# Two output blocks of a fused FFN: copied out of PSUM by ScalarE and added to x by the transfer out

## The chip, the cores and the metric

The kernel runs on one core of a Trainium2 chip. The core has a matrix engine (TensorE, PE in the profile; PEld is its weight load), a vector engine (VectorE, DVE), a scalar engine (ScalarE, ACT), a general engine (GpSimd, POOL) and SyncE (SP), which here only issues DMA transfers. The metric is device time in microseconds: 259.87 us before, the median of three runs (259.43 to 259.95).

## The reference

`x` is 64 batches of 64 rows of 512 numbers, all in 32 bits. Cut to what matters, the reference computes

```
q   = relu(cond @ W3 + b3)                      # 64 x 512, one row a batch
v   = (64 * x + sum of x over the batch's rows) * q
y   = relu(v @ W2 + b2)
out = x + y @ W_base + b_base + (y @ A_s) @ B_s + sum over e of w_e * (y @ A_r[e]) @ B_r[e]
```

Here `w_e` are the two largest of six softmax gates of `y @ W_router + b_router`, the others being zero. The `x +` at the front of `out` is what the change is about.

## The kernel before

The 4096 rows of x are cut into four blocks (k = 0 to 3) of 1024 rows. Everything is held transposed: features on the 128 partitions, rows along the free axis. One block passes through these stages: modulation of x to v, first matmul (W2) to y, a matmul `ph` (L1066) for gates and low-rank factors, and the second matmul (W_base) with the routed part added, then the transfer out.

Both large matmuls use Strassen-Winograd products: a block's matrix is split in two by two, so that seven products (`prod` with numbers 1 to 7) replace eight. In the second matmul, `second` (L658), sums of products accumulate in PSUM banks named x, y, z and w, each with two columns j = 0 and 1 of 128 features. Four result blocks come out: C12 and C22 (features 256 to 511) begin as `with_x("y", ...)` and `with_x("z", ...)`, where DVE adds rows of x to a bank into an SBUF tile, and are completed by `leave` (L690) from bank w. C11 (bank x) and C21 (bank z), features 0 to 255 of the two halves of the rows, are complete in their banks once `routed` (L682) has added the routed part, and leave through `finish` (L687), which is called four times a block.

The rows of x to be added come from `load_rows` (L648): it loads four tiles of 128 x 2 x 512 numbers, 512 KB each, with transfers issued by SP. The tiles have the tags u21, u, u22 and u12, with one buffer each. u22 holds the rows of C11 and u12 those of C21. The same four tags are the scratch tiles of the first matmul (`temps`, L60): in `first_inner` (L431), which does the first matmul of blocks 1 to 3, tag u is p1, u22 is p5, u21 is u and u12 is v7. So the first writer of p5 in block k + 1, the second of the two copies by ACT at L468, waits until the transfers out of u22 in block k are done.

The order of work is written out by hand: each engine runs its instructions in the order in which the code issues them, with waits on semaphores set in between. While block k is in its second matmul, the modulation of block k + 1 (L218 on ACT, with sums on DVE) is handed out from the list `behind` by `share` (L698), nine times in `second`. The counts in `share` hand out all of the modulation's activations by the fourth call, which precedes the first `finish`; the later calls give out DVE's row sums (L269 to L272) and inner sums (L307 to L310), which the next block's first matmul reads. POOL computes `hwd` (L604) from the routed factors, then the steps of `beside[k]` (L1028 in block 0, four additions of `inner_tb` in block 1, eight in block 2), and in the next block the sums `inner_two` and `inner_late` (L307, L550).

The last block's second matmul is another function, `second_inner` (L759), with its own ways out.

Of the kernel before, what the change touches and what calls it, by code (L numbers as in the profile page):

```python
# [11 lines left out]
ALU = mybir.AluOpType  # L12
# [7 lines left out]
TB = 512  # L20
NB = T // (2 * TB)
# [4 lines left out]
KH = NC // 2  # L26
# [11 lines left out]
def adaln_ffn(ctx: ExitStack, tc: tile.TileContext, xa, x0, x1, head, w3, w2, wb, a, bcat, bb, br, outT):  # L38
# [8 lines left out]
    nc = tc.nc  # L47
# [126 lines left out]
    def product(ps, i, j, w, s, start=True):  # L174
        for c in range(KH):
            nc.tensor.matmul(  # L176
                ps, w[i][:, c, ts(j, P)], s[i][:, c, :], start=start and c == 0, stop=c == KH - 1,
                skip_group_check=True,
            )
# [99 lines left out]
    def fill(n):  # L279
        for _ in range(min(n, len(behind))):  # L280
            for step in behind.pop(0):
                step()
# [301 lines left out]
    def weigh(k, ph):  # L584

        nc.vector.tensor_tensor(
            hw[:, :, :GR].rearrange("p s (g r) -> p s g r", r=R),
            ph[:, :, :GR].rearrange("p s (g r) -> p s g r", r=R),
            w.unsqueeze(3).to_broadcast([P, 2 * NS, G, R]),
            ALU.mult,  # L590
        )

    def turn(k):
        pt = ps_h.tile([P, 2 * NS, P], F32, tag="ph", name=f"pt_{k}")
        hwT = small.tile([P, 2, TB], F32, tag="hwT", name=f"hwT_{k}")
        for s in range(2 * NS):
            nc.tensor.transpose(pt[:GB, s, :], hw[:, s, :], ident)  # L597
        for h in range(2):
            nc.scalar.copy(hwT[:GB, h], pt[:GB, ts(h, NS)].rearrange("p s t -> p (s t)"))  # L599
        return hwT  # L600

    def difference(k, hwT):
        hwd = small.tile([P, TB], F32, tag="hwd", name=f"hwd_{k}")
        nc.gpsimd.tensor_tensor(hwd[:GB], hwT[:GB, 0], hwT[:GB, 1], ALU.subtract)  # L604
        return hwd
# [42 lines left out]
    def load_rows(k):  # L648

        res = {}  # L650
        for n, (f, h) in zip(pair_tags[2:3] + pair_tags[:2] + pair_tags[3:], ((1, 0), (1, 1), (0, 0), (0, 1))):
            res[f, h] = tmp.tile([P, KH, TB], F32, tag=n, name=f"x{n}_{k}")
            nc.sync.dma_start(
                res[f, h], x1[k, f * KH : (f + 1) * KH, :, ts(h, TB)].rearrange("c p t -> p c t")
            )
        return res

    def second(k, y, ph, res):  # L658

        sy = sys_[k]  # L660
        ps = {}

        def bank(name, j):
            ps[name, j] = ps_p.tile([P, TB], F32, tag="pp", name=f"o{name}_{k}_{j}")
            return ps[name, j]

        def prod(i, j, name, start=True):
            product(bank(name, j) if start else ps[name, j], i, j, tb, sy, start=start)

        def seed(name, source, j):  # L670
            nc.scalar.copy(bank(name, j), ps[source, j])

        def row(f, h):
            return res[f // KH, h][:, f % KH]

        def with_x(name, j, f, h):

            t = row(f, h)
            nc.vector.tensor_tensor(t, ps[name, j], t, ALU.add)
            return t  # L680

        def routed(name, j, f, hw):  # L682
            nc.tensor.matmul(  # L683
                ps[name, j], bcat_sb[:, ts(f, P)], hw, start=False, stop=True, skip_group_check=True
            )

        def finish(name, j, f, h):  # L687
            nc.sync.dma_start(outT[k, f, h], with_x(name, j, f, h))

        def leave(p, f, h, add):  # L690
            nc.vector.tensor_tensor(add, p, add, ALU.add)
            nc.sync.dma_start(outT[k, f, h], add)


        places = list(range(9, 0, -1))
        most = {9: 4, 8: 5, 7: 6}

        def share():  # L698
            n = places.pop(0)
            left = len(behind) - 13  # L700
            fill(min(left, most.get(n, 6)) if left > 0 else -(-len(behind) // n))

        gate(k, ph)
        prod(1, 0, "x")
        seed("y", "x", 0)
        prod(1, 1, "x")
        seed("y", "x", 1)
        prod(6, 0, "y", start=False)
        seed("z", "y", 0)
        prod(2, 0, "x", start=False)  # L710
        weigh(k, ph)
        u12, u22 = {}, {}
        u12[0] = with_x("y", 0, KH, 0)
        share()
        prod(7, 0, "z", start=False)
        u22[0] = with_x("z", 0, KH, 1)
        prod(6, 1, "y", start=False)
        seed("z", "y", 1)
        u12[1] = with_x("y", 1, KH + 1, 0)
        share()  # L720
        prod(2, 1, "x", start=False)
        prod(7, 1, "z", start=False)
        u22[1] = with_x("z", 1, KH + 1, 1)
        hwT = turn(k)
        hwd = difference(k, hwT)
        for step in beside[k]:
            step()
        share()
        prod(4, 0, "z", start=False)
        prod(5, 0, "w")  # L730
        share()
        routed("x", 0, 0, hwT[:GB, 0])
        finish("x", 0, 0, 0)
        routed("z", 0, 0, hwT[:GB, 1])
        finish("z", 0, 0, 1)

        routed("w", 0, KH, hwT[:GB, 1])
        leave(ps["w", 0], KH, 1, u22[0])
        share()
        prod(5, 1, "w")  # L740
        routed("w", 1, KH + 1, hwT[:GB, 1])
        leave(ps["w", 1], KH + 1, 1, u22[1])
        share()
        routed("x", 1, 1, hwT[:GB, 0])
        finish("x", 1, 1, 0)
        share()
        prod(4, 1, "z", start=False)
        routed("z", 1, 1, hwT[:GB, 1])
        finish("z", 1, 1, 1)
        share()  # L750
        prod(3, 0, "w", start=False)
        routed("w", 0, KH, hwd[:GB])
        leave(ps["w", 0], KH, 0, u12[0])
        share()
        prod(3, 1, "w", start=False)
        routed("w", 1, KH + 1, hwd[:GB])
        leave(ps["w", 1], KH + 1, 0, u12[1])
# [280 lines left out]
    for k in range(NB):  # L1038
# [6 lines left out]
        if k == 1:  # L1045
            wide_sums()
        res = load_rows(k)
        if k == 0:
            load_x(3)
# [79 lines left out]
```

## Time and profile before

The profiled execution took 259.86 us; its span on the core is 258.1 us.

| | before |
|---|---|
| profiled execution, us | 259.86 |
| span, us | 258.1 |
| TensorE busy, us | 252.6 |
| VectorE busy, us | 199.6 |
| ScalarE busy, us | 142.7 |
| GpSimd busy, us | 68.8 |
| mean granted TensorE clock | 0.997 |
| additions of x from PSUM (L679): number, us each | 24, 0.68 |
| stores of `finish` (L688): number, us to landing | 12, 2.0 |
| loads of `load_rows` (L653): number, us to landing | 16, 3.7 |

Blocks begin their first matmul on TensorE at 73.2 (block 1), 134.8 (block 2) and 196.3 us (block 3), and their second at 41.4, 102.8 and 164.3 us (blocks 0 to 2). Busy shares are averages over stages with different limits; where an engine waits, the profile names what ended the wait.

### The profile page before, as it was taken

The numbers are of one execution on the slowest core, as the hardware profiler recorded it, in microseconds if no ns is written. First come the engines' busy times: TensorE is split into PE (matmuls) and PEld (weight loads), VectorE is DVE, ScalarE is ACT, GpSimd is POOL, SyncE is SP. The second block draws the span as 40 slices with busy tenths as digits, with TensorE's granted clock in tenths as the row PEclk, the third lists the DMA queues.
The fourth block names the chain that finished last, engine by engine and source line by source line (L and its number), as shares of the span: only waits on it lengthen the run. The fifth ranks groups of instructions, "written<-read, shape, count | busy, mean of one in ns | idle before, by whom it ended". The sixth has DMA issues, their size and how long they took to land.

```text
span 258.1 us, 3326 instructions
## 1 busy us (share of the span) xinstructions
PE 252.6 (98%) x1034; PEld 170.6 (66%) x1034; DVE 199.6 (77%) x404; ACT 142.7 (55%) x391; POOL 68.8 (27%) x88
## 2 busy tenths in 40 slices
PE   7999999999999999999999999999999999999994
PEld 3755896454468889445448888744446889975783
DVE  2899898789958976967995894996896476887473
ACT  2399587597037897279106889439603527443220
POOL 1000000012008520005104650000920864039950
PEclk9999999999999999999999999999999999999998
DMA  6998729403320035000431023300232003600054
GB/s 174 369 341 297 290 79 379 192 3 122 122 81 0 4 143 183 0 3 0 163 123 41 0 83 118 130 0 3 104 140 81 0 6 128 193 1 3 0 183 142
DMA packets 14675, 28.54 MB, mean 111 GB/s; under 512 B 1489, under 2 KB 3537, under 8 KB 14658
## 3 DMA queue, kind: packets, MB, share of 16 engines
q1 hardware_dynamic: 14370, 28.08, 30.9%
q10 hardware_dynamic: 288, 0.26, 0.3%
q8 instruction: 8, 0.13, 0.2%
q14 instruction: 9, 0.07, 0.1%
HBM read 19.94 MB, written 8.39 MB: 110 GB/s over the span
## 4 chain that ended last, share of the span: by engine, by line
PE 94%; ACT 2%; DMA 2%; SPq 0%; issue 0%; DVE 0%
PE ia L453 13%; PE ph L1066 11%; PE ib L453 10%; PE oz L176 9%; PE ox L176 8%; PE ow L176 8%; PE py L361 5%; PE oy L176 5%; PE ja L820 4%; PE ow L683 4%; PE jb L820 4%; PE ox L683 2%; PE oz L683 2%; DMA w_sb<-in_w_dram 2%; PE yw L176 1%; PE pt L597 1%
## 5 line engine op out<-in xcount | busy, mean ns | idle before, releaser
L218 ACT ACTIVATE x<-x,vsum,nq 128x64 f32<-128x64 f32 x192 | 67.5, 431 | 6.8 <-DVE vsum L214 6.8
L604 POOL TENSOR_TENSOR hwd<-hwT 113x512 f32<-113x512 f32 x4 | 5.6, 1393 | 109.4 <-ACT hwT L599 109.4
L1066 PEld LDWEIGHTS ph<-a_sb,y 128*128 128x128 f32 x256 | 30.3, 192 | 1.3 <-ACT y L347 0.7
L1066 PE MATMUL ph<-a_sb,y 128*128 128x118 f32 x256 | 30.8, 276 | 0.3 <-ACT y L347 0.3
L459 ACT COPY ib<-ia 128x256 f32<-128x256 f32 x21 | 7.6, 361 | 42.3 <-PE ia L453 42.3
L444 DVE TENSOR_TENSOR u<-ib,u 128x256 f32<-128x256 f32 x42 | 16.4, 418 | 18.6 <-PE ib L453 18.5
L176 PE MATMUL ox<-y,wb_sb 128*128 128x512 f32 x48 | 22.1, 593 | 0.0
L444 DVE TENSOR_TENSOR u<-ia,u 128x256 f32<-128x256 f32 (+1 forms) x36 | 16.1, 461 | 2.9 <-ACT u L491 1.6
L347 ACT ACTIVATE y<-u,head_sb 128x256 f32<-128x256 f32 (+1 forms) x30 | 15.8, 584 | 3.8 <-DVE u L419 3.1
L453 PE MATMUL ib<-inner_s,inner_t 128*128 128x256 f32 x60 | 17.8, 384 | 0.0
L213 DVE TENSOR_REDUCE vsum<-x 128x8 f32<-128x512 f32 x24 | 16.2, 675 | 0.0
L176 PEld LDWEIGHTS ox<-y,wb_sb 128*128 128x128 f32 x48 | 8.9, 190 | 10.0 <-issue 9.6
L176 PE MATMUL oz<-sy,tb 128*128 128x512 f32 x32 | 15.2, 599 | 0.0
L361 PE MATMUL py<-v,w_sb 128*128 128x512 f32 (+1 forms) x40 | 14.4, 510 | 0.8 <-DMA w_sb<-in_w_dram 0.8
L176 PE MATMUL oy<-sy,tb 128*128 128x512 f32 x32 | 14.9, 594 | 0.0
L307 POOL TENSOR_TENSOR inner_two<-x 128x256 f32<-128x256 f32 x3 | 2.2, 727 | 45.0 <-PE ib L453 45.0
L462 ACT COPY ib<-ib 128x256 f32<-128x256 f32 x21 | 7.6, 363 | 9.9 <-PE ib L453 9.9
L453 PEld LDWEIGHTS ib<-inner_s,inner_t 128*128 128x128 f32 x60 | 11.2, 190 | 2.2 <-ACT ib L462 0.8
L256 ACT ACTIVATE v<-x,vsum,nq 128x64 f32<-128x64 f32 x32 | 11.0, 430 | 1.9 <-DVE vsum L254 1.9
L361 PEld LDWEIGHTS py<-v,w_sb 128*128 128x128 f32 x40 | 7.4, 190 | 6.5 <-issue 4.5
L176 PE MATMUL oz<-y,tb 128*128 128x512 f32 x24 | 11.3, 592 | 0.0
L176 PE MATMUL ow<-sy,tb 128*128 128x512 f32 x24 | 11.3, 592 | 0.0
(236 smaller groups left out, 545.0 us busy)
## 6 DMA issues: line engine op xcount, KB each, us to landing
xu<-in_x_dram SPq DMA_DIRECT2D x16, 512.0 KB, 3.7
out_dram<-xu SPq DMA_DIRECT2D x29, 256.0 KB, 2.0
x<-in_x_dram SPq DMA_DIRECT2D x12, 512.0 KB, 7.6
x<-in_x_dram SPq DMA_DIRECT2D x7, 256.0 KB, 5.6
w_sb<-in_w_dram SPq DMA_DIRECT2D x4, 256.0 KB, 5.6
wb_sb<-in_wb_dram SPq DMA_DIRECT2D x4, 256.0 KB, 4.8
out_dram<-xu SPq DMA_DIRECT2D x4, 128.0 KB, 1.7
w_sb<-in_w_dram SPq DMA_DIRECT2D x1, 384.0 KB, 5.2
```

Of the source, the lines that this page charges most:

```text
L176: nc.tensor.matmul(ps, w[i][:, c, ts(j, P)], s[i][:, c, :], start=start and c == 0, stop=c == KH - 1, skip_group_check=True,)
L213: nc.vector.tensor_reduce(vsum[:, c, bs], xc, AX.XY, ALU.add)
L218: nc.scalar.activation(x, x, AF.Identity, bias=vsum[:, c, b : b + 1], scale=nq[:, c, b : b + 1])
L256: nc.scalar.activation(v[:, c, :, ts(b, NH)], batches_of(c, b, b + 1)[:, :, 0], AF.Identity, bias=vsum[:, c, b : b + 1], scale=nq[:, c, b ...
L347: nc.scalar.activation(y[:, f, h, cols], src, AF.Relu, bias=b2_sb[:, f : f + 1])
L361: nc.tensor.matmul(p[:, :, lo * NH : hi * NH], w2_sb[:, c, ts(f, P)], v[:, c, :, lo * NH : hi * NH], start=(c == 0 and lo == 0), stop=(c = ...
L444: add = lambda o, a, b: nc.vector.tensor_tensor(o, a, b, ALU.add)
L453: nc.tensor.matmul(bank[b, t][:, cols], t_side(o, n), s_side(o, n), start=n == 1, stop=True, skip_group_check=True,)
L459: nc.scalar.copy(bank["b", t][:, lo], bank["a", t][:, lo])
L683: nc.tensor.matmul(ps[name, j], bcat_sb[:, ts(f, P)], hw, start=False, stop=True, skip_group_check=True)
L820: nc.tensor.matmul(p, w, s, start=start, stop=True, skip_group_check=True)
L1066: nc.tensor.matmul(ph[:, h * NS + s, :HC], y[:, c, h, ts(s, P)], a_sb[:, c, :], start=(c == 0), stop=(c == NC - 1),)
```

## The change

For blocks 0 to 2, `load_rows` no longer loads the rows of x for C11 and C21 into SBUF. SP issues a transfer from x in DRAM to their place in the output in DRAM instead; the two SBUF tiles are still allocated. `finish` has ACT copy the bank into the tile, and POOL issues a transfer that adds the tile to what stands in the output. The other two result blocks, and block 3, are as before.

```
@@ load_rows
             res[f, h] = tmp.tile([P, KH, TB], F32, tag=n, name=f"x{n}_{k}")
+            if f == 0 and k < NB - 1:
+
+                nc.sync.dma_start(outT[k, :KH, h], x1[k, :KH, :, ts(h, TB)])
+                continue
             nc.sync.dma_start(
                 res[f, h], x1[k, f * KH : (f + 1) * KH, :, ts(h, TB)].rearrange("c p t -> p c t")
             )
@@ second
         def finish(name, j, f, h):
-            nc.sync.dma_start(outT[k, f, h], with_x(name, j, f, h))
+            t = row(f, h)
+            nc.scalar.copy(t, ps[name, j])
+            nc.gpsimd.dma_start(outT[k, f, h], t, accum_op=ALU.add)
```

## The prediction

> **What bounds the kernel now.** I read the page's first two parts, then the chain of waits, busy time by stretches, the list of who waited for whom, and last the timeline of ScalarE (ACT), VectorE (DVE) and GpSimd (POOL) around the end of a block. The page first:
>
> ```profile
> span 258.1 us, 3326 instructions
> PE 252.6 (98%) x1034; PEld 170.6 (66%) x1034; DVE 199.6 (77%) x404; ACT 142.7 (55%) x391; POOL 68.8 (27%) x88
> PE 94%; ACT 2%; DMA 2%; SPq 0%; issue 0%; DVE 0%
> ```
>
> TensorE (PE) is busy nearly all the time, and the chain that ended last runs through it for 94% and through DVE for 0%. Shares are averages, so next the stretches of block 1's inner product and of its second matmul, and the last 18 us of the second matmul of blocks 0, 1 and 2 (columns: length, then busy time of each engine, with the number of instructions):
>
> ```profile
> 73.21:102.76 29.55, 29.39 (x164) 25.48 (x163) 21.81 (x47) 23.60 (x66) 10.61 (x12) 1.00 0.23 83
> 102.76:134.75 31.99, 31.99 (x82) 14.46 (x81) 27.31 (x52) 14.06 (x39) 4.67 (x5) 1.00 0.16 58
> ...
> 57.00:75.00 18.00, 18.00 (x47) 8.52 (x46) 17.28 (x24) 6.78 (x22) 2.56 (x2) 1.00 0.27 102
> 118.80:136.50 17.70, 17.70 (x47) 8.38 (x46) 15.88 (x22) 5.46 (x17) 4.67 (x5) 1.00 0.28 104
> 180.40:198.00 17.60, 17.60 (x46) 8.27 (x46) 16.08 (x22) 5.39 (x17) 7.75 (x9) 1.00 0.28 104
> ```
>
> Where the change sits, PE has no idle time at all; DVE is nearly full beside it (17.28 of 18.00), ACT is not (6.78). A full DVE costs only if PE waits for it (us in total, times, longest):
>
> ```profile
> ACT ib L459 <- PE ia L453: 42.3, 15, 12.0
> DVE u L444 <- PE ib L453: 18.5, 13, 2.8
> PEld oz L176 <- ACT oz L671: 1.5, 2, 0.7
> PEld ow L176 <- DVE xu L679: 0.5, 2, 0.2
> ```
>
> The first two lines are engines waiting for PE: ACT idles up to 12.0 us and DVE up to 2.8 us at a block's start. The last is the only wait of PE's weight loads for the additions that go: 0.24 us each, the same gap that the loads beside them show as issue. It costs nothing.
>
> Last, the timeline of ACT, then POOL, where the new copies and transfers will go, and where the next block needs their tile (start, length):
>
> ```profile
> 57.02 6.08 ACT L218 ACTIVATE x<-x,vsum,nq 128x64 f32<-128x64 f32 x18
> 74.11 0.36 ACT L459 COPY ib<-ia 128x256 f32<-128x256 f32 x1 [11.01 <-PE ia L453]
> 75.25 0.38 ACT L468 COPY u<-ia 128x256 f32<-128x256 f32 x1
> 75.98 0.37 ACT L476 COPY u<-ib 128x256 f32<-128x256 f32 x1 [0.36 <-PE ib L453]
> ...
> 187.57 0.90 POOL L170 TENSOR_TENSOR inner_tb<-wb_sb,inner_tb 128x128 f32<-128x128 f32 x1
> 200.54 0.73 POOL L307 TENSOR_TENSOR inner_two<-x 128x256 f32<-128x256 f32 x1 [12.06 <-PE ib L453]
> ```
>
> ACT is empty from 63.10 to 74.11; POOL in the worst block is free from 188.47 to 200.54.
>
> **Removed: twelve DVE additions.** Four in each of blocks 0 to 2 (L679 from `finish`), 0.68 us each, one every 0.60 us when they follow each other: 4 x 0.60 = 2.4 us of DVE a block. None is on the path: before its first work of the next block DVE waits 2.66 us (block 0) or 2.77 us (block 1) for PE, so the 2.4 us lengthen that wait. Worth 0. Bounds: a loss is excluded, since nothing is added to DVE's queue; the gain is at most what PE loses to DVE early in an inner product, weight-load waits of 1.0 us in four and 0.6 us in two for u L444, 0.24 us of each being the ordinary gap, so 1.6 - 6 x 0.24 = 0.2 us.
>
> **Added: twelve ACT copies from PSUM.** The nearest row is the seed copy of the same shape, 0.57 us: 2.3 us a block. `share()` hands out all modulation work before the first `finish` (18 instructions up to 63.10 in block 0, 14 up to 123.61 and 185.14 in the others), so nothing of it queues behind a copy that waits for PE. Block 0: first column of C11 copied 63.10 to 63.67, of C21 to 64.2; second columns when PE ends them, at 65.47 and 68.05, so to 66.1 and 68.7. Cover: ACT's hole of 11 to 12 us; without it, 2.3 us a block. PSUM: the w accumulators reuse the y banks, which DVE empties as before; the banks emptied by the new copies are wanted again only from 73.2. Worth 0.
>
> **Moved: twelve transfers out, from SP's queue to POOL's, as accumulations.** SP loses 12 issues of 0.34 us; nobody waits for SP there, and its other four transfers go out no later. POOL gains 12 issues that wait for the copies. Ahead of them stand hwd and the `beside` steps, behind them the next block's inner_two: at 77.46 in block 0, at 200.54 in block 2. No row of before shows an issue by POOL: at least SP's 0.34 us, at most POOL's longest instruction in this stage, 1.44 us (hwd L604); I take 1.17 us (L1028, POOL's instruction of 256 elements), as POOL's own work is the nearest kind. In block 2 four issues end at 188.47 + 4.7 = 193.2, or 194.2 at the upper bound: before 200.54. Worth 0.
>
> **The new wait.** Tile u22 holds C11 and becomes p5 of the next block: the second ACT copy of L468 (75.25, 136.78, 198.32) may not write it before the second C11 accumulation has read it out and landed. It stood behind a plain store that landed in 2.0 us. Behind it on ACT queue L476 and the seed L462, for which PE waits, so lateness beyond ACT's 0.36 us hole is PE's. Tile u12 (C21) is wanted some 4 us later still.
>
> How long does an accumulation take? No row shows one. The nearest are the transfers of the page (KB each, us from issue to landing) and the rate from 30 to 50 us, in 40 slices:
>
> ```profile
> xu<-in_x_dram SPq DMA_DIRECT2D x16, 512.0 KB, 3.7
> out_dram<-xu SPq DMA_DIRECT2D x29, 256.0 KB, 2.0
> ```
>
> ```profile
> GB/s 213 8 16 25 0 0 0 0 0 0 0 0 0 90 74 332 397 369 410 361 369 348 311 307 311 389 418 430 426 418 418 401 426 418 410 279 188 82 8 0
> ```
>
>  It reads 256 KB from SBUF and 256 KB from DRAM, and writes 256 KB. While eight 512 KB loads ran together (36 to 48 us) the rate was about 418 GB/s: 0.63 us for 256 KB. A plain store lands in 2.0 us, so 1.4 us is latency. Lower bound: like the store, 2.0 us, overlapping. Upper: a 512 KB load (3.7 us) and a store (2.0 us) in sequence, three in a row without overlap, 17.1 us. I take the two reads at the measured rate, 1.3 us each in sequence, and 1.4 us latency once: three take 5.3 us. The stream of 512 KB loads is nearest, because these transfers too are 2 KB rows spread over the same 16 engines and follow each other.
>
> Landing, counted from the end of the first issue: block 0, 64.84 + 5.3 = 70.1 against 75.25; block 1, 124.18 + 1.17 + 5.3 = 130.7 against 136.78; block 2, 188.47 + 1.17 + 5.3 = 194.9 against 198.32. All hidden, by 5.1, 6.1 and 3.4 us. Block 2 gives way first: above (198.32 - 1.4 - 189.64) / 3 = 2.4 us a transfer. At the upper bound lateness is 6.7, 5.7 and 8.4 us: 20.8 less 3 x 0.36, some 20 us: 280 us.
>
> The Trainium skill has a rule against this: "SBUF — State Buffer", section "SBUF: two separate sides", warns that a transfer issued by GpSimd can be starved of descriptors while DVE holds the shared port pair, and a later section prices one at about 3.1 us where 0.62 us was alone. The trace has a neighbour of it: L272 on DVE took 1.75 us beside POOL's hwd where it takes 0.68 us otherwise. By the rule, an estimate, three transfers would come 7.4 us later, and block 2 would lose 4 us; but the same page exempts DVE's two-input additions, and those fill the stretch here.
>
> **Copies of x into DRAM.** They replace two of SP's four loads of 512 KB a block (0.39 us an issue, 3.7 us to land); nothing computes from them until the accumulation 20 us later (issued by 99.55 at the latest in block 1, first used at 124.2). They no longer wait for a tile. At the load's price they are hidden; at a load and a store in sequence, 5.7 us, too. In block 0 the load of x_3 queues behind them, which is used two blocks later. Worth 0.
>
> **End of the program.** SP closes by waiting for every queue's semaphores; the accumulations add up to eight, at 17 to 38 ns each: 0 to 0.3 us. I take 0.05 us, as SP waits 1.8 us for the last store anyway.
>
> **Sum.** Profiled execution 259.86 us (span 258.1, 1.76 around it), the median of three being 259.87: + 0 + 0 + 0 + 0.05 = 259.9 us.
>
> **Rivals.**
> 1. *The accumulations land late and hold ACT at the block's start* (slower; decides above 2.4 us a transfer). For: three 256 KB streams and an adder that no row prices, and issues that start as late as 188.47. Against: 3.4 us of room. At 3.0 us a transfer block 2 is 189.64 + 9.0 + 1.4 - 198.32 - 0.36 = 1.4 us late and blocks 0 and 1 not: 261.3 us. At 3.25 us block 2 is 2.1 us late and block 0 0.4 us: 262.4 us.
> 2. *POOL's first transfer has a starting cost.* For: POOL issues none before. Against: room of 5.1 us in block 0. It shows from 5.1 + 0.36 + 0.5 = 6 us on: 260.4 us.
> 3. *DVE's relief reaches PE.* For: DVE 96% busy at 57 to 75. Against: DVE waits for PE right after. At most 0.2 us by the row above, 259.7 us; to be told from no change it needs a third of PE's 1.5 us wait for ACT's oz seeds as well, which lie ahead of the change's place: 259.2 us.
> 4. *ACT becomes late.* Were modulation behind the copies, up to 2.3 us a block, 266.8 us; its order excludes that.
>
> **How the numbers follow.** About 0.2% (0.5 us) is what a measurement of this kernel tells from no change. Hidden as summed, 0.49 (own range 259.4 to 260.3); rival 1, 0.27; rival 2, 0.06; rival 3, 0.13; rival 4 and other slowings, 0.05. Of the three slower cases' 0.38, 0.02 stays under 0.5 us: slower 0.36, same 0.51, faster 0.13. The range runs to where 1 in 10 is left above (3.25 us a transfer, 262.4 us) and below (259.3 us).
>
> **What would show it.** L679 x12 instead of x24 on DVE and its wait before block starts longer by about 2 us; twelve ACT copies right after the last L218; landing of accumulations under 5 us; the second L468 still 1.14 us after L459 begins. Wrong, if an ACT wait for a transfer appears at L468, if POOL's inner_two starts later than PE lets it, or if PE's stretches of 31.98 us or 29.55 us change.

## The result, and the profile after

The changed kernel takes 260.53 us (median of seven, 260.27 to 261.25), the kernel before beside it 259.87 us (259.35 to 260.24): a ratio of 1.0031 [1.0016, 1.0046]. The change makes the kernel slower by 0.3%, a little more than measurements of it can tell from no change (the interval leaves 1 out by 0.0016). The profiled execution took 260.44 us.

The page of the changed kernel first: span, busy time, engines on the chain that ended last, then two groups and the transfers.

```profile
span 258.7 us, 3333 instructions
...
PE 252.4 (98%) x1034; PEld 170.5 (66%) x1034; DVE 193.0 (75%) x392; ACT 149.1 (58%) x403; POOL 79.3 (31%) x100
...
PE 92%; ACT 2%; DVE 2%; DMA 2%; SPq 0%; issue 0%
...
L694 POOL DMA_DIRECT2D out_dram<-xu x12 | 10.7, 1016 | 11.5 <-ACT xu L693 8.8
...
out_dram<-xu SPq DMA_DIRECT2D x17, 256.0 KB, 2.3
out_dram<-in_x_dram SPq DMA_DIRECT2D x6, 512.0 KB
out_dram<-xu POOLq DMA_DIRECT2D x12, 256.0 KB, 5.1
```

The work moved as the diff says: DVE lost twelve instructions and 6.6 us, ACT gained 6.4 us. PE is as full as before, and DVE, which was on 0% of the chain, is on 2%. Busy time by stretches: block 1's inner product, its second matmul, then block 2's inner product and its second matmul, and last the end of block 0's second matmul.

```profile
72.92:102.53 29.61, 29.45 (x164) 25.49 (x163) 21.29 (x47) 23.60 (x66) 10.59 (x12) 1.00 0.17 60
102.53:134.53 32.00, 32.00 (x82) 14.45 (x81) 25.26 (x48) 16.18 (x43) 8.18 (x9) 1.00 0.36 83
134.53:164.52 29.99, 29.56 (x163) 25.48 (x163) 21.67 (x47) 23.66 (x66) 10.59 (x12) 1.00 0.16 55
164.52:196.51 31.99, 31.99 (x81) 14.45 (x81) 25.60 (x48) 16.19 (x43) 11.22 (x13) 1.00 0.31 73
57.00:75.00 18.00, 18.00 (x48) 8.60 (x47) 14.85 (x20) 8.84 (x25) 6.14 (x6) 1.00 0.71 179
```

The second matmuls, where the new copies and accumulations run, are what they were (31.99 us before). In the last row DVE fell from 17.28 to 14.85 us of 18.00 with no effect on PE. The inner products are longer, the first from 29.55 to 29.61 us, the second from 29.55 (134.75 to 164.30 before) to 29.99 us.

The chain of both kernels says where three pieces of time lie. The one before:

```profile
73.21 2.30 PE ia L453 x10
...
134.75 2.30 PE ia L453 x10
...
196.28 2.30 PE ia L453 x10
...
252.10 1.73 PE ja L820 x8
```

and the one after:

```profile
72.92 2.36 PE ia L453 x10
...
134.53 2.36 PE ia L453 x10
...
196.51 2.36 PE ia L453 x10
...
252.38 1.73 PE ja L826 x8
```

- **Block starts**: the first group of matmuls of blocks 1 to 3 takes 2.36 us instead of 2.30: 3 x 0.06 = 0.18 us.
- **Block 2's inner product**: 0.44 us longer, of which 0.06 is the group just named: 0.38 us.
- **The end**: from the start of the last group of matmuls to the end of the span, 258.1 - 252.10 = 6.0 us before, 258.7 - 252.38 = 6.3 after: 0.3 us.

Together 0.86 us. In this pair of executions the profile shows only 0.6 us, because the first loads happened to be 0.28 us quicker: the first `ph` matmul starts at 33.99 us, at 34.27 before. That start moves between executions, up to 36.6 us in those below, so from here on kernels are compared by these three pieces beside the medians.

What the prediction was most afraid of isn't there. The second copy of L468 in block 2 and the accumulation that it must wait for, first L694 with its landing, then L468 (ACT's own waits are the first line of it):

```profile
L694 POOL DMA_DIRECT2D out_dram<-xu x2: 1184/1360/1535, 189.2 to 189.8; - x2
...
DMA to landing us min/median/max: 5.8/6.2/6.6
```

```profile
L468 ACTq EVENT_SEMAPHORE  x3: 17/17/38, 197.5 to 198.4; - x3
L468 ACT COPY u<-ia x2: 378/378/379, 197.7 to 198.6; 128x256 f32<-128x256 f32 x2
```

Issued at 189.77, landed 6.57 us later at 196.3, wanted at 198.6: 2.3 us to spare, and no waiting instruction of ACT longer than 38 ns. The room differs between executions: in a second run of the same kernel (e1 below) this accumulation was issued at 189.9, landed at 197.6 and was wanted at 198.7, with 1.1 us to spare. The landing of it and of the transfer issued just ahead of it there:

```profile
DMA to landing us min/median/max: 6.9/7.3/7.7
```

### The profile page after: what moved, and what is told of

Same layout as the page of the kernel before. It is cut to its first block, busy times and chain, and to the rows that moved or that the text cites. A ratio compares the mean times of both kernels' runs of the same rounds, so it can differ in the third digit from the quotient of the medians.

```text
span 258.7 us, 3333 instructions
## 1 busy us (share of the span) xinstructions
PE 252.4 (98%) x1034; PEld 170.5 (66%) x1034; DVE 193.0 (75%) x392; ACT 149.1 (58%) x403; POOL 79.3 (31%) x100
## 4 chain that ended last, share of the span: by engine, by line
PE 92%; ACT 2%; DVE 2%; DMA 2%; SPq 0%; issue 0%
PE ia L453 12%; PE ph L1072 11%; PE oz L176 9%; PE ib L453 9%; PE ox L176 8%; PE ow L176 8%; PE py L361 5%; PE oy L176 5%; PE ja L826 4%; PE ow L687 4%; PE jb L826 4%; PE oz L687 2%; PE ox L687 2%; DMA w_sb<-in_w_dram 2%; PE yw L176 1%; PE pt L597 1%
## 5 line engine op out<-in xcount | busy, mean ns | idle before, releaser
L444 DVE TENSOR_TENSOR u<-ib,u 128x256 f32<-128x256 f32 x42 | 16.4, 420 | 20.2 <-PE ib L453 20.0
L459 ACT COPY ib<-ia 128x256 f32<-128x256 f32 x21 | 7.6, 360 | 23.8 <-PE ia L453 23.6
L444 DVE TENSOR_TENSOR u<-ia,u 128x256 f32<-128x256 f32 (+1 forms) x36 | 16.2, 463 | 2.9 <-ACT u L491 1.6
L697 DVE TENSOR_TENSOR xu<-ow,xu 128x512 f32<-128x512 f32 x12 | 8.3, 688 | 8.2 <-PE ow L687 8.2
L694 POOL DMA_DIRECT2D out_dram<-xu x12 | 10.7, 1016 | 11.5 <-ACT xu L693 8.8
```

The costliest lines, as they stand in the source:

```text
L444: add = lambda o, a, b: nc.vector.tensor_tensor(o, a, b, ALU.add)
L694: nc.gpsimd.dma_start(outT[k, f, h], t, accum_op=ALU.add)
```

## The experiments

Two ideas stood against each other at first. One: the time goes to the accumulating transfers or to their contention. The other: it goes to what comes along with them, more semaphores, more waiting instructions, another order. All kernels are compared by the three pieces; the last two columns set the sum of what they exceed (2.30, 29.55 less the first piece's share, 6.0 us) beside the difference of the medians. "Before" is the kernel before on the same chip. The ratios in the text, each with its 95% interval, are not the quotients of the medians and differ from them by up to 0.0016.

| kernel | median, us | before, us | first group | block 2's inner product | end | pieces sum | medians |
|---|---|---|---|---|---|---|---|
| e1 the change again | 260.52 | 259.70 | 2.36 | 29.97 | 6.3 | +0.8 | +0.8 |
| e2 before, 8 small POOL transfers | 260.01 | 259.70 | 2.30 | 29.57 | 6.0 | +0.1 | +0.3 |
| e3 before, stores by POOL | 260.31 | 259.70 | 2.30 | 29.91 | 6.3 | +0.7 | +0.6 |
| e4 ACT copies, no x | 259.82 | 259.70 | 2.36 | 29.62 | 5.9 | +0.1 | +0.1 |
| e5 change, one memset more | 260.08 | 259.67 | 2.36 | 29.62 | 6.3 | +0.5 | +0.4 |
| e6 before, ten memsets more | 259.97 | 259.67 | 2.30 | 29.90 | 6.0 | +0.4 | +0.3 |
| e7 change, copies of x split | 259.87 | 259.67 | 2.36 | 29.63 | 5.9 | +0.2 | +0.2 |
| e8 change, plain stores | 260.52 | 259.67 | 2.36 | 29.95 | 6.3 | +0.8 | +0.9 |
| e9 e7, C21 copied by DVE | 259.88 | 259.59 | 2.36 | 29.63 | 5.9 | +0.1 | +0.3 |
| e10 e7, ACT copies j = 1 only | 259.64 | 259.71 | 2.30 | 29.56 | 5.9 | 0.0 | -0.1 |
| e11 e7, ACT copies j = 0 only | 259.79 | 259.71 | 2.36 | 29.61 | 5.9 | +0.1 | +0.1 |

Except in e2 and e9, 0.2 us apart, the pieces account for the medians within 0.1 us.

### e1: the change once more

> The changed kernel once more, for a second profile. Theory A (three small terms): slower than before by 0.3 us of closing waits, 3 x 0.06 us at the starts of blocks 1 to 3 where ACT's seed copy L459 got a wait of its own, and up to 0.4 us where POOL's L550 and DVE meet in block 2. From ACT's last issue to the end of the span 2.9 us again (before 2.5); L459 starts 0.96 us after TensorE's first ia (before 0.90). If the meeting in block 2 is a matter of chance, L550 starts 0.57 us after the DVE group in some profiles and 0.94 us in others. 260.5 us. Theory B (the accumulations are late): ACT waits at L468; the first result showed no such wait, so B expects none here either and has to say where else.

260.52 us, ratio 1.0016 [0.9997, 1.0034]: the interval takes in 1, so by the time alone this run would not show a loss. By the trace it does: the same three pieces, and the 0.4 us in the same place of block 2 again: it belongs to the kernel, not to one execution.

### e2: eight small transfers on GpSimd in the kernel before

```
+    small_sb = const.tile([P, 8, E], F32, tag="small_sb", name="small_sb")
...
     beside = {
         0: [lambda: nc.gpsimd.tensor_tensor(bcat_d, ...)]
+        + [lambda n=n: nc.gpsimd.dma_start(small_sb[:, n], br.partition_broadcast(P)) for n in range(8)]
     }
```

> The kernel before, with eight transfers of 3 KB issued by POOL beside block 0's second matmul, read by nobody: as many semaphores of POOL's transfers as the change has, and nothing else of it. Theory A1 (the end costs by the number of semaphores to wait for): +0.3 us, 260.2 us. Theory A2 (it costs by how many of SP's closing waits come after the one for the last transfer; here that wait is the seventh of nine, with two behind it as before): +0.05 us, 259.9 us.

260.01 us, ratio 1.0005 [0.9982, 1.0029], no verdict by the median. By the pieces: the end is 6.0 us, not 6.3, though SP closes with 11 semaphore instructions here as in the changed kernel and POOL's clearing of the semaphores takes as long (139 ns, 96 in the kernel before). What differs is the place of the last transfer in SP's closing list: in the compiled program two entries of nine stand behind its entry here, six of nine in the changed kernel, two of five in the kernel before. So it isn't the length of the list alone.

### e3: GpSimd issues the plain stores, DVE still adds

```
-            nc.sync.dma_start(outT[k, f, h], with_x(name, j, f, h))
+            nc.gpsimd.dma_start(outT[k, f, h], with_x(name, j, f, h))
```

> The kernel before, with the twelve transfers of finish issued by POOL as plain stores; DVE adds x as before, no copies into DRAM, no copies by ACT. The last transfer's wait is the third of nine at the end, with six behind it, as in the changed kernel. A1 and A2: +0.3 us, 260.2 us, from ACT's last issue to the end 2.9 us. Theory B (only accumulation costs): 259.9 us.

260.31 us, ratio 1.0019 [1.0004, 1.0034]. Two pieces are there without any accumulation, ACT copy or copy of x: block 2 (29.91 us) and the end (6.3 us). The block starts are clean (2.30).

### e4: the ACT copies alone

```
+            if f == 0 and k < NB - 1:
+                continue
...
-            nc.sync.dma_start(outT[k, f, h], with_x(name, j, f, h))
+            t = row(f, h)
+            nc.scalar.copy(t, ps[name, j])
+            nc.sync.dma_start(outT[k, f, h], t)
```

> ScalarE copies C11 and C21 out as in the change, but SP stores the tiles plainly and x is not added to C11 and C21 of blocks 0 to 2 (left out, neither loaded nor copied). No transfer by POOL. Theory A: L459's own wait at three block starts, +0.18 us, and an end slightly shorter than before (the last transfer's wait is the last): 260.0 us. If ACT's copies cost nothing at all: 259.8 us. If DVE's relief is worth something to TensorE: below 259.4 us.

259.82 us, ratio 0.9997 [0.9981, 1.0012]. The counterpart of e3: block starts at 2.36 us, the rest clean. DVE's twelve additions are gone here and nothing came of it.

### e5: one memset more in the changed kernel

Block 2's loss, looked at closely, begins in one pair of POOL instructions. The list of L550 in the changed kernel, 146 to 149 us (durations in ns, start of the first to start of the last):

```profile
L550 POOL TENSOR_TENSOR inner_late<-u,u x2: 1276/1276/1277, 147.2 to 148.4; 128x512 f32<-128x512 f32 x2
L550 POOLq EVENT_SEMAPHORE  x1: 17/17/17, 146.7 to 146.7; - x1
```

and in the kernel before:

```profile
L550 POOL TENSOR_TENSOR inner_late<-u,u x2: 1262/1266/1270, 147.0 to 148.2; 128x512 f32<-128x512 f32 x2
L550 POOLq EVENT_SEMAPHORE  x1: 17/17/17, 146.9 to 146.9; - x1
```

Before, the addition starts 0.1 us after the semaphore instruction (one that only waits) in front of it; after the change 0.5 us, though both kernels have the same waits there, on the same VectorE and ScalarE instructions. In blocks 1 and 3 it is 0.1 us in both kernels. The semaphore came on time; the instruction came late. That made theory F: POOL gets its 69th recorded instruction (counted in the trace, those that only wait or issue among them) late, and the transfers only moved L550 to that place.

```
-    nc.gpsimd.memset(tri, 0.0)
+    for _ in range(2):
+        nc.gpsimd.memset(tri, 0.0)
```

> The changed kernel with one more instruction on GpSimd, a memset of the small tile tri at the start, which takes 0.1 us beside the first loads. Theory F: the 0.44 us that block 2's first inner product lost lies between GpSimd's semaphore instruction and the addition behind it (L550), 0.46 us apart instead of 0.11, because GpSimd gets its 69th recorded instruction late; one instruction more in front moves the late place off this pair, the first inner product of block 2 is back at 29.6 us, and the time is 260.1. Theory C: it is the transfers on GpSimd's queue that disturb this place; one memset at the start changes nothing, 29.97 us and 260.5.

260.08 us, 0.44 less than the change in e1; ratio to the kernel before 1.001 [0.9995, 1.0024]. Block 2's inner product is back at 29.62 us. One instruction of 0.1 us at the start of the program removes the loss. Theory F holds, C falls.

### e6: ten memsets more in the kernel before

```
-    nc.gpsimd.memset(tri, 0.0)
+    for _ in range(11):
+        nc.gpsimd.memset(tri, 0.0)
```

> The kernel before with ten more memsets of the small tile tri on GpSimd at the start, no transfer from GpSimd. They put as many recorded instructions in front of block 2's L550 as the changed kernel has. Theory F, if a transfer counts as one instruction: block 2's first inner product goes from 29.55 to about 29.95 us and the time to 260.2. If a transfer counts as several, the late place falls elsewhere and the time stays at 259.9. Theory C: no transfers, no delay, 259.9 and 29.55 us.

259.97 us, ratio 1.0004 [0.9986, 1.0021]: too close to tell by the time. The trace tells: 29.90 us for block 2's inner product, 29.55 for block 1's, and the pair is apart without any transfer by POOL (lines are one further on in this kernel, so L551 is L550):

```profile
L551 POOL TENSOR_TENSOR inner_late<-u,u x2: 1270/1271/1272, 146.8 to 148.1; 128x512 f32<-128x512 f32 x2
L551 POOLq EVENT_SEMAPHORE  x1: 17/17/17, 146.4 to 146.4; - x1
```

How 0.35 us on POOL, which is far from full, reaches PE can be followed in the timelines (start, length). The kernel before:

```profile
146.96 2.49 POOL L550 TENSOR_TENSOR inner_late<-u,u 128x512 f32<-128x512 f32 x2 [2.19 <-DVE u L444]
...
147.83 0.43 DVE L212 TENSOR_SCALAR nq<-q_sb 128x16 f32<-128x16 f32 x1
...
151.00 0.30 PEld L453 LDWEIGHTS ia<-x,t 128*128 128x128 f32 x2 [0.30 <-DVE u L444]
```

The changed kernel:

```profile
147.17 2.50 POOL L550 TENSOR_TENSOR inner_late<-u,u 128x512 f32<-128x512 f32 x2 [2.58 <-DVE u L444]
...
147.67 0.81 DVE L212 TENSOR_SCALAR nq<-q_sb 128x16 f32<-128x16 f32 x1
...
151.21 0.30 PEld L453 LDWEIGHTS ia<-x,t 128*128 128x128 f32 x2 [0.67 <-DVE u L444]
```

DVE's small L212 (median 0.17 us) ends 0.03 us after the first of POOL's two additions ends, in both: 146.96 + 1.27 = 148.23 and 147.83 + 0.43 = 148.26 before, 147.17 + 1.28 = 148.45 and 147.67 + 0.81 = 148.48 after. POOL later by 0.35 us makes L212 longer by 0.38 us, everything on DVE behind it comes as much later, and PE's wait for DVE's u (L444) grows from 0.30 to 0.67 us. The chain of the changed kernel runs through DVE at this place, where that of the kernel before has no DVE; it is most of the 2% on the page:

```profile
146.23 1.52 DVE u L444 x4
147.75 0.73 DVE nq L212
148.48 0.60 DVE vsum L213
```

The Trainium skill, "SBUF — State Buffer", section "SBUF: two separate sides", says of the port pair that DVE and GpSimd share that it is an exclusive lock: whoever starts first keeps it for its whole instruction. L212 ending with POOL's instruction agrees with that; the additions L444, one of whose two inputs lies in PSUM and which ran beside the same L550 at their usual 0.41 us, were not held.

### e7: the copies of x split in two

```
-                nc.sync.dma_start(outT[k, :KH, h], x1[k, :KH, :, ts(h, TB)])
+                for c in range(KH):
+                    nc.sync.dma_start(outT[k, c, h], x1[k, c, :, ts(h, TB)])
```

> The changed kernel with each copy of x in DRAM cut in two of 256 KB. Nothing of the work changes, but six more transfers on SP make the last transfer out fall on the last entry of SP's closing list of waits instead of the third of nine. Theory L (the closing waits behind the last transfer cost some 0.06 us each): from the last group of matmuls to the end of the span 6.30 us becomes 5.95, the time 260.2. Theory N (it is the number of waits and of semaphores to clear that costs, wherever the last transfer stands): 6.3 us and 260.5 stay. Twelve issues of half the size on SP hide as six do.

259.87 us, ratio 1.0003 [0.9988, 1.0018]. The chain's last group and SP's closing semaphores in this kernel, whose span is 257.8 us:

```profile
251.82 1.73 PE ja L827 x8
```

```profile
L1131 SPq EVENT_SEMAPHORE  x11: 17/28/28, 254.7 to 257.7; - x11
```

257.75 (the span to two places) - 251.82 = 5.9 us with eleven semaphore instructions. Theory L holds: it costs what stands behind the last transfer. With none of nine entries behind it, 5.9 us (e7, e9 to e11), with two of nine 6.0 (e2), with six of nine 6.3 (the change, e3, e5, e8): about 0.06 us an entry. The traces show these entries one by one. SP's list from the entry that the last landing released, first the kernel before, then the changed one:

```profile
L1124 SPq EVENT_SEMAPHORE  x3: 28/28/28, 257.1 to 257.3; - x3
```

```profile
L1130 SPq EVENT_SEMAPHORE  x7: 27/28/28, 257.4 to 257.8; - x7
```

Each starts 0.06 us after the one in front of it; four more make 0.24 us, and the longer clearing 0.04, together the 0.3 us. The time fell by more than was expected, because the new transfers also put four more semaphore instructions on POOL's queue, L550 of block 2 is the 73rd recorded instruction instead of the 69th, and the loss there is gone as in e5. Twelve copies in DRAM cost nothing visible beside six.

### e8: no accumulation

```
-            nc.gpsimd.dma_start(outT[k, f, h], t, accum_op=ALU.add)
+            nc.gpsimd.dma_start(outT[k, f, h], t)
```

> The changed kernel with plain transfers out by GpSimd in place of the accumulating ones, so that x is left out of C11 and C21 of blocks 0 to 2. If the accumulation costs nothing on the path, as the trace after says, 260.5 us with the same three stretches (2.36 us for the first group of each later block, 29.97 us for block 2's first inner product, 6.3 us at the end). If accumulation disturbs other transfers or the end, the time falls below 260.3. The transfers' own landing goes from 5.1 us to about 2.

260.52 us, ratio 1.0034 [1.0016, 1.0052]: the time of the changed kernel, all three pieces included. The transfers land in 2.9 us (median) where the accumulations take 5.1, and none of these 2.2 us is on the path.

### e9, e10 and e11: what lengthens the block starts

In the changed kernel the seed copy L459, by which ACT copies the first `ia` half of a bank to `ib`, starts 0.96 us after PE's first matmul of the block, before 0.90. The list of L459 from 72.5 to 75.6 us, changed kernel (the kernel before has no semaphore instruction there, only the two copies):

```profile
L459 ACTq EVENT_SEMAPHORE  x2: 17/17/17, 73.8 to 74.7; - x2
L459 ACT COPY ib<-ia x2: 357/357/357, 73.9 to 74.7; 128x256 f32<-128x256 f32 x2
```

The bank that becomes `ib` was last read by ACT itself, in `finish`. In the compiled program the copy now has two waits, one for PE and one for ACT's own count, and the first sits in an instruction of its own, the semaphore instruction of the list. To tell that from ACT's being busier, some of the four copies went to DVE (from the kernel e7, so that the other pieces stay out):

```
             t = row(f, h)
-            nc.scalar.copy(t, ps[name, j])
+            if name == "x":
+                nc.scalar.copy(t, ps[name, j])
+            else:
+                nc.vector.tensor_copy(t, ps[name, j])
             nc.gpsimd.dma_start(outT[k, f, h], t, accum_op=ALU.add)
```

> The kernel of the split copies with one edit: the two banks z of C21 are copied out of PSUM by VectorE, those of C11 still by ScalarE, all four still accumulated by GpSimd. The banks z are the ones that the first two ib banks of the next block take over. Theory W (the first group of a later block takes 2.36 us for 2.30 because ScalarE's seed copy into ib must wait for ScalarE's own copy out of that bank, one more waiting instruction in the chain): the group is back at 2.30 us in all three blocks, the lag of the seed copy at 0.90 us, and the time 0.18 us lower, 259.7 us where the split copies gave 259.87. Theory A (it comes from ScalarE being busier with copies): six copies fewer leave it at about 2.33 us and 259.8. VectorE's six copies more cost nothing in either.

259.88 us, ratio 1.0009 [0.9992, 1.0025], and 2.36 us as before: a miss, and no verdict. With this edit the first `ib` takes a bank of C11 rather than of C21, so that ACT's own wait stood there again. e10 has the condition `j == 1`, e11 `j == 0`:

> The kernel of the split copies; ScalarE copies out the second bank of C11 and C21 (j = 1) and VectorE the first (j = 0), GpSimd accumulates all four. In the compiled program the first seed copy of a block then waits for TensorE alone, the second one for ScalarE's own copy too. Theory W (one more waiting instruction ahead of the first seed copy is the 0.06 us): lag 0.90 us and a first group of 2.30 us in all three blocks, 259.7 us. Theory A (it comes with ScalarE's copies, whichever they are): 0.96 and 2.36 us as with the split copies.

> The same the other way round: ScalarE copies out the first bank (j = 0), VectorE the second. As many copies on each engine as in the run with j = 1, but the first seed copy now waits for ScalarE's own copy and the second does not. Theory W: lag 0.96 and a first group of 2.36 us, some 0.18 us in all above the run with j = 1. Theory A: the same times as that run.

Six copies by each engine in both. L459 at the start of block 1 and the chain's first groups in e10:

```profile
L459 ACT COPY ib<-ia x2: 357/357/357, 74.9 to 75.8; 128x256 f32<-128x256 f32 x2
L459 ACTq EVENT_SEMAPHORE  x1: 17/17/17, 75.8 to 75.8; - x1
```

```profile
74.02 2.30 PE ia L453 x10
...
135.57 2.30 PE ia L453 x10
...
197.13 2.30 PE ia L453 x10
```

and in e11:

```profile
L459 ACT COPY ib<-ia x2: 357/357/357, 75.9 to 76.7; 128x256 f32<-128x256 f32 x2
L459 ACTq EVENT_SEMAPHORE  x1: 17/17/17, 75.9 to 75.9; - x1
```

```profile
74.97 2.36 PE ia L453 x10
...
136.57 2.36 PE ia L453 x10
...
198.18 2.36 PE ia L453 x10
```

In e10 the semaphore instruction stands ahead of the second copy (75.8) and the groups take 2.30 us, in e11 ahead of the first (75.9) and they take 2.36. Theory W holds: the instruction is the 0.06 us. The times are 259.64 us, ratio 0.9994 [0.9976, 1.0012], and 259.79 us, ratio 0.9989 [0.9967, 1.0012]; the difference of the medians, 0.15 us, is what 3 x 0.06 would give but is less than these times can tell. e10 is the change with all three pieces taken out (six of the twelve copies are DVE's there). Its time cannot be told from that of the kernel before.

## Why the prediction was right or wrong

The range held the time (260.53 in 259.3 to 262.4), but the likeliest case, all hidden and within 0.5 us of before, did not come about: 0.66 us. Slower had 0.36, nearly all of it for mechanisms that didn't act. That the range held is luck: its upper end was set by late accumulations, which held up nothing, and the 0.66 us come from three terms that the sum put at 0 or 0.05.

- **Twelve DVE additions, worth 0**: right. e10 and e4 have six and twelve fewer and gain nothing. The place of the relief was misread: DVE's longest wait for PE at a block start grew from 2.8 to 3.2 us, not by about 2 us; most of it went into waits for PE ahead of the additions of `leave` (L697: 8.2 us in six waits, 0.3 us in two before).
- **Twelve ACT copies, worth 0**: wrong by 0.18 us. They do fit into ACT's hole, and PE never waits for one. The step asked only when the emptied banks are wanted again, not what the taking over adds: one semaphore instruction in the chain PE, ACT, PE, 0.06 us at each of three block starts (e10 against e11).
- **Twelve POOL issues, worth 0**: wrong by 0.38 us, though the durations were inside the bounds (0.86 us for most, 1.54 at most, against 1.17 taken) and POOL was in time for inner_two. Their number cost, not their length: with eight transfers and their waits in front, L550 of block 2 fell on an instruction that POOL gets 0.35 us late (e5, e6). That is also the prediction's own sign of error: the stretch of 29.55 us changed.
- **The new wait at L468, hidden**: right, with the size off. Three accumulations of block 2 took 6.8 us from the end of the first issue (189.5) to 196.3, not 5.3; 2.3 us were to spare, not 3.4, and 1.1 us in e1. The other two blocks had 3.4 and 4.2 us. One input was read too high: the row of GB/s stands near 418 only from 43 to 47 us, and between 307 and 410 from 37.5 to 42.5. Landings under 5 us were forecast; their median is 5.1. The rule of the skill on starved descriptors would have made it 7.4 us later than forecast; it came 1.4 us later, 2.7 in e1.
- **Copies of x in DRAM, worth 0**: right, for six and for twelve (e7), though not at the price assumed: SP took 0.6 to 5.2 us to issue one (median 2.7), not the load's 0.39. In block 0 the load of x_3 was issued from 42.5 us on, 37.7 before, and nothing waited for it. The page gives no landing time for these copies.
- **The end, 0.05 us**: the mechanism was right and the size wrong, 0.3 us, the upper bound of the step. It took SP's wait for the last store as cover for the whole list; it covers only the entries ahead of the last transfer's, and six stood behind, at 0.06 us each, where two did before.
- **Rivals**: 1 (late accumulations) fell, no wait of ACT shows; 2 (a starting cost of POOL's first transfer) too, the first accumulation landed in 4.5 us; 3 (DVE's relief reaches PE) fell by e4 and e10; 4 (ACT late) fell as it was put, the 0.06 us of L459 being a wait of another kind.

Sum of what the runs showed: 0.18 + 0.38 + 0.3 = 0.86 us, against 0.8 between the medians in e1 and 0.66 in the result.

## What to carry to other kernels

Work that moves behind other work is free only in its duration: ask also how many instructions and waits it puts ahead of a chain that passes between engines, who last read the bank that such a chain takes over, and where the last transfer stands in the closing list. When a difference of a few tenths of a microsecond sits far from the edit, compare each instruction's start with the semaphore instruction in front of it, and shift the queue by one harmless instruction: if the loss goes, it belonged to the place and not to the work. And a relief of an engine that waits for the bound one is worth nothing, however full it looks beside it.

## What the runs showed of the hardware that was not expected

- **A late instruction.** At one place of POOL's queue, about its 69th recorded instruction in these kernels, an instruction starts 0.35 us later after its wait than the same instruction in blocks 1 and 3. It was seen in the change, e1, e3, e6 and e8; in e2 it fell, by 0.36 us, on the semaphore instruction behind L550's first addition, where POOL was busy and nothing was lost. In the changed kernel the only transfer between 146 and 149 us is one of an instruction queue:

```profile
DMA packets 1, 0.01 MB, mean 3 GB/s; under 512 B 0, under 2 KB 0, under 8 KB 0
...
q14 instruction: 1, 0.01, 1.0%
```

  The same packet follows the late L550 in e1, e3, e6 and e8, and neither the kernel before nor e5 has any packet in this stretch. So a change-over in the loading of POOL's program is the likely cause; the runs show the place and the company, not the cause. The Trainium skill, "Runtime: NRT & Kernel Launch", section "Instruction fetch mechanics", says that engines fetch their program in blocks while they run and that crossing from one to the next is mostly hidden. Here the 0.35 us showed in the five runs in which L550 of block 2 fell on that place, and were hidden in e2.
- **The price of a place in the closing list**: about 0.06 us for each entry behind the last transfer's (5.9 us from the last group of matmuls to the end with none behind, 6.3 with six).
- **Accumulating transfers**: 256 KB added in DRAM land 4.3 to 6.6 us after issue by POOL (4.0 to 7.7 in e1), plain stores by POOL in 2.4 us (median, e3) and 2.9 us (e8), plain stores by SP in 2.0 (before).
